# Eight instead of six expert blocks begun before the routing is complete, and their closing sums rearranged over VectorE, ScalarE and GpSimd

## The chip, the cores and the metric

The kernel runs on one core of a Trainium2 chip. The metric is the time of one execution on the device in microseconds. Lower is better. Engines are named as the profile names them: PE is TensorE's matmul side (PEld its weight loads), DVE is VectorE, ACT is ScalarE, POOL is GpSimd, SP is SyncE, which here only issues DMAs.

## The reference, cut to what matters

The reference is a two-layer decoder over x of shape (32, 100, 256), each sub-layer followed by a layer norm. The part that matters here is the last sub-layer, a mixture of eight experts over the 3200 tokens, and the layer norm behind it:

```python
logits = x_flat @ Wg + bg                      # (3200, 8)
probs = jax.nn.softmax(logits, axis=-1)
assignments = jnp.argmax(probs, axis=-1)       # one expert a token
h = jax.nn.gelu(jnp.einsum('nd,edh->neh', x_flat, W1) + b1[None], approximate=False)
eo = jnp.einsum('neh,ehd->ned', h, W2) + b2[None]
selected = jnp.take_along_axis(eo, assignments[:, None, None], axis=1)[:, 0, :]
w = jnp.take_along_axis(probs, assignments[:, None], axis=1)
out = (w * selected).reshape(N, T, d)
...
x = _layernorm(x + out)                        # no gain, no bias
```

## The kernel before, in words

The attention part (two layers, 32 batches each) runs from a plan written out by hand: `at(slot, place, do)` puts a piece of work into a numbered slot, and `run_slots` (L911) issues the slots in order. What is issued in one order stays in that order on each engine (only at the seam between the two contexts, the attention part and the block loop, do instructions of the second slip in between the last of the first). The slots of the last layer end at 347.

While attention still runs, the rows of a batch whose routing is done are scattered by GpSimd to `regions`, a DRAM buffer with room per expert. The experts then work on blocks of 128 rows that belong to one expert. There are 32 blocks (`BLOCKS` = 3200/128 + 7). `BEGUN` = 6 of them are begun early, from what 24 batches have sent (`BEGIN_WITH`): `begun_rows` and `begun_experts` (L860, L870) read their places and experts into registers, `load_begun` (L874) loads rows and first matrix, and `BEGINNING` (L36) gives for each the slot in which its rows are turned (`turn_rows`, two PE transposes and an ACT copy) and the slot of its first matrix (`first_matrix`, eight matmuls and two ACT additions of a bias). The first matrix of the last begun block is left to `end_begun`.

After the last slot come, still in the first context: the load of ACT's table for gelu (L1000), `table_of_others` (the table with the places of the remaining blocks, which SP waits for before it loads them), `end_begun` (L893: for each begun block a gelu on ACT and the second matrix on PE, four matmuls into one of four PSUM banks), and `sum_begun` (L902). For each begun block that calls `share_and_residual` (L135), four DVE instructions:

- L138 adds the expert's second bias and empties the PSUM bank,
- L139 multiplies by the token's share and adds the residual row,
- L141 and L142 make mean and variance.

`margin` (L145, POOL) adds 1e-05 to the variance, `scale` (L148, POOL) takes the power -1/2, `shift_of` (L151, DVE) makes minus mean times that, `normalise_on_scalar` (L1049, ACT) normalises a block with it; `normalise` (L1053, through L154, DVE) does the same on VectorE. `store` scatters the 128 finished rows to the output by an indirect DMA that POOL issues (L779).

The remaining 26 blocks go through a loop (L1061) as a pipeline: in step i the load of block i+10 is issued, the rows of block i+2 are turned, the first matrix of i+1 and its gelu run, block i-3 is normalised on ACT, the second matrix of i and its sums run, and block i-3 is stored. On ACT the order of a step is therefore: copy of turned rows (i+2), gelu (i+1), normalisation (i-3). In the step before the first of these, L1066 puts the ACT normalisations of the begun blocks 0 to 2, after the gelu of the first other block and ahead of the copy for the third. Begun blocks 3 to 5 are normalised on DVE in the steps 8 to 10. At the end of the loop, POOL issues the stores of blocks 26 to 28, then the margin and power of the last pair, then the stores of 29 to 31.

Of the kernel before, what the change touches and what calls it, by code (L numbers as in the profile page):

```python
# [11 lines left out]
I32 = mybir.dt.int32  # L12
# [6 lines left out]
E = 8  # L19
P = 128  # L20
# [13 lines left out]
FILLS = 23  # L34
BEGUN, BEGIN_WITH = 6, 24
BEGINNING = (((338, 1), (340, 2)), ((338, 3), (342, 1)), ((339, 1), (343, 3)), ((339, 3), (345, 2)), ((340, 1), (346, 0)), ((341, 1), None))  # L36
NO_TOKEN = 1000000
# [29 lines left out]
def decoder_kernel(ctx: ExitStack, tc: tile.TileContext, a: dict, out: bass.AP):  # L67
# [66 lines left out]

    def share_and_residual(i, ps, pool):  # L135
        t = blocks[i]
        y = t["y"]
        nc.vector.tensor_tensor(y, ps, b2[:, bass.ds(t["e"], 1), :].rearrange("p o d -> p (o d)"), ALU.add)  # L138
        nc.vector.scalar_tensor_tensor(y, y, t["x"][:, D:D + 1], t["x"][:, :D], ALU.mult, ALU.add)  # L139
        st = pool.tile([P, 6], F32, tag="st", name=f"st_{i}")  # L140
        nc.vector.bn_stats(st, y)  # L141
        nc.vector.bn_aggr(mv_all[:, i, :], st)  # L142

    def margin(i, n):
        nc.gpsimd.tensor_scalar_add(rs_all[:, i:i + n], mv_all[:, i:i + n, 1], 1e-05)  # L145

# [14 lines left out]
    with ExitStack() as att:  # L161
# [649 lines left out]

        def write_table(name, upto, skips, firsts):

            past = sm.tile([32, E - 1], F32, tag="tb_past", name=f"{name}_past")
            col = sm.tile([32, 2], F32, tag="tb_col", name=f"{name}_col")
            nc.vector.tensor_scalar(past, upto[:32, :E - 1], c["steps"][:32, 1:2], None, ALU.is_le)
            nc.vector.tensor_reduce(col[:, 1:2], past, AX.X, ALU.add)
            skips = skips()
            nc.vector.tensor_tensor_reduce(past, past, skips[:32, :E - 1], 1.0, firsts[:32, :], ALU.mult, ALU.add, col[:, 0:1])
            nc.vector.tensor_copy(rows_by_block[:, 0:64:32], col)  # L820
            nc.vector.transpose(table, rows_by_block)

        def table_of_begun():

            assert BEGIN_WITH * S - E * (P - 1) > (BEGUN - 1) * P
            u = {}

            def counts():
                u["n"], u["upto"] = blocks_of_experts("begun", 0.5 / P - 0.5, None)

            def whole_blocks():
                n, upto = u["n"], u["upto"]
                nc.vector.tensor_scalar(upto, upto, float(BEGUN), None, ALU.min)
                nc.vector.tensor_copy(done[:, 0:1], upto[:, 0:1])
                nc.vector.tensor_tensor(done[:, 1:], upto[:, 1:], upto[:, :E - 1], ALU.subtract)
                nc.vector.tensor_scalar(n, done, -float(P), float(B * S), ALU.mult, ALU.add)

            def rows():
                write_table("begun", u["upto"], lambda: u["n"], c["steps"][:, 0:1])

            def for_others():
                nc.vector.tensor_tensor(over, done[:, 1:], done[:, :E - 1], ALU.subtract)
                nc.vector.tensor_scalar(over, over, float(P), float(B * S), ALU.mult, ALU.add)
                nc.vector.scalar_tensor_tensor(first_done, done[:, 0:1], float(P), c["steps"][:, 0:1], ALU.mult, ALU.add)
            return counts, whole_blocks, rows, for_others

        def table_of_others():

            n, upto = blocks_of_experts("counts", 0.5 - 0.5 / P, done)

            def skips():
                nc.vector.scalar_tensor_tensor(n[:, :E - 1], n[:, :E - 1], -float(P), over, ALU.mult, ALU.add)
                return n
            write_table("counts", upto, skips, first_done)

# [4 lines left out]
        def begun_rows():  # L860
            firsts = of_table(0, BEGUN, 0, (ENG.SP,), (BLOCKS_AT_MOST - 1) * P)
            experts = of_table(0, BEGUN, 1, (ENG.SP,), E - 1)
            for i, (first, e) in enumerate(zip(firsts, experts)):
                t = blocks[i]
                t["first"], t["e"], t["ident"] = first, e, ident
                t["x"], t["y"] = x_all[:, i, :], x_all[:, BEGUN + i, :D]
                t["hT"], t["xT"] = slot_of(2 * BEGUN + i), slot_of(3 * BEGUN + i)
                t["w"] = w1_begun[:, i, :]
# [32 lines left out]

        def sum_begun():  # L902
            for i in range(BEGUN):
                share_and_residual(i, blocks[i]["ps"], sm)
                if i == BEGUN // 2 - 1:
                    margin(0, BEGUN // 2)
                    scale(0, BEGUN // 2)
                if i == BEGUN // 2:
                    shift_of(0, BEGUN // 2)

# [91 lines left out]
        end_begun()  # L1002
        sum_begun()

    with ExitStack() as moe:
# [3 lines left out]
        ps_m = moe.enter_context(tc.tile_pool(name="ps_m", bufs=2, space=bass.MemoryType.PSUM))  # L1009
        m16 = moe.enter_context(tc.tile_pool(name="m16", bufs=16))  # L1010
        m12 = moe.enter_context(tc.tile_pool(name="m12", bufs=12))
# [3 lines left out]
        for i in range(BEGUN, BLOCKS):  # L1015
            blocks[i]["y"] = y_all[:, i - BEGUN, :]

# [24 lines left out]
        def second_layer(i):  # L1042
            ps = bank(f"bo_{i}")[:, :D]
            second_matrix(blocks[i], ps, shared)
            share_and_residual(i, ps, m4)

# [7 lines left out]

        def store(i):
            scatter("out", out=out.rearrange("b s d -> (b s) d"),
                    out_offset=bass.IndirectOffsetOnAxis(ap=blocks[i]["x"][:, D + 1:].bitcast(I32), axis=0), in_=blocks[i]["y"],
                    bounds_check=B * S - 1, oob_is_err=False)

        half = BEGUN // 2  # L1060
        for i in range(BEGUN - 10, BLOCKS):  # L1061
# [3 lines left out]
            if i == BEGUN - 1:  # L1065
                for j in range(half):  # L1066
                    normalise_on_scalar(j)
                    store(j)
            if i < BEGUN:
                continue  # L1070
            if i > BEGUN + 2:
                normalise_on_scalar(i - 3)
            second_layer(i)
            if i == BLOCKS - 1:
                normalise_on_scalar(i - 2)
                store(i - 3)
            if i == BEGUN + 1:
                margin(half, half)
                scale(half, half)
            if i % 2:  # L1080
                margin(i - 1, 2)
                scale(i - 1, 2)
            elif i > BEGUN:
                shift_of(i - 2, 2)
            if BEGUN + 1 < i < BEGUN + 2 + half:
                normalise(i - 2 - half)
                store(i - 2 - half)
            if BEGUN + 2 < i < BLOCKS - 1:
                store(i - 3)
        store(BLOCKS - 3)  # L1090
# [73 lines left out]
```

## Time and profile before

| | us |
|---|---|
| three runs | 1735.86, 1736.29, 1737.64 (median 1736.29) |
| the profiled execution, its own time | 1733.78 |
| its span in the profile | 1731.8 |
| PE busy in it | 1678.4 (97%) |
| DVE, POOL, ACT busy | 1296.1, 1096.8, 911.9 |
| stretch behind the last slot, to the last POOL instruction | 1655 to 1725.7 |

The profile is one execution of the program. Its times are counted from the start of the span. A row of the timeline gives start, duration, engine, line, operation and tiles; a bracket at its end says how long the engine had been idle and what ended the wait. The table of windows gives busy time by engine in a stretch, and after them the granted TensorE clock (1.00 is full speed) and the busy share and rate of DMA.

### The profile page before, as it was taken

Reading aid. Unit: us, or ns where it says so; the run is one execution under the profiler, and the core shown is the slowest. Engines: PE = TensorE matmul, PEld = TensorE weight load, DVE = VectorE, ACT = ScalarE, POOL = GpSimd, SP = SyncE. Lnnn points to the kernel's source line nnn. Section 1 sums busy time; section 2 is a strip of 40 time slices with the busy share of each in tenths; the row PEclk is TensorE's granted clock in tenths of the full one; section 3 lists DMA queues with packets and bytes.
Section 4 is the critical chain, followed back from the end, with each engine's and each line's share of the span. In section 5 each row is a group of like instructions: output and inputs, shape, how many; then the busy total and the mean of one; then the engine's idle time right before and its main releaser. Section 6 shows DMA issues by size and latency. Waiting matters only on the chain.

```text
span 1731.8 us, 52249 instructions
## 1 busy us (share of the span) xinstructions
PE 1678.4 (97%) x20803; PEld 1298.7 (75%) x20803; DVE 1296.1 (75%) x3803; ACT 911.9 (53%) x2255; POOL 1096.8 (63%) x1655
## 2 busy tenths in 40 slices
PE   8999999999999999999999999999999999999996
PEld 6777777777777777776777777777777777777685
DVE  5677877777787777787767787877777777786775
ACT  3455555555555555555445555555555555554554
POOL 1566676666667666666336777676766767675657
PEclk9999999999999999999999999999999999999998
DMA  4001322332332233121421131010000000021063
GB/s 161 15 22 31 82 66 64 83 85 50 85 82 65 65 82 85 45 53 31 135 90 55 55 104 47 29 29 19 27 13 22 26 19 20 19 72 56 11 202 123
DMA packets 64048, 104.90 MB, mean 61 GB/s; under 512 B 6108, under 2 KB 43486, under 8 KB 63679
## 3 DMA queue, kind: packets, MB, share of 16 engines
q1 hardware_dynamic: 59790, 94.44, 19.9%
q0 software_dynamic: 3584, 6.59, 1.2%
q8 instruction: 165, 2.70, 0.7%
q14 instruction: 77, 0.62, 0.1%
q10 hardware_dynamic: 432, 0.54, 0.1%
HBM read 61.32 MB, written 41.13 MB: 59 GB/s over the span
## 4 chain that ended last, share of the span: by engine, by line
PE 78%; DVE 14%; POOL 3%; issue 2%; DMA 1%; ACT 0%; POOLq 0%; SPq 0%; DVEq 0%; ACTq 0%
PE r_t_x L435 13%; PE sc_x L341 10%; PE r_k L536 8%; PE r_v L545 7%; PE r_a_x L450 6%; DVE pr L421 6%; PE r_t_s L392 4%; PE r_o_x L364 3%; POOL pr L425 3%; PE r_o_s L364 3%; PE r_qx L321 3%; PE sc_s L341 2%; PE r_a_s L399 2%; DVE pr_s L382 2%; DVE mx_s L379 2%
## 5 line engine op out<-in xcount | busy, mean ns | idle before, releaser
L425 POOL TENSOR_TENSOR pr<-pr,mx_x 100x361 f32<-100x361 f32 x992 | 766.2, 802 | 230.8 <-DVE mx_x L421 223.1
L436 ACT ACTIVATE pT_x<-r_t_x 120x400 f32<-120x400 f32 (+1 forms) x768 | 371.0, 503 | 268.0 <-PE r_t_x L435 265.8
L435 PEld LDWEIGHTS r_t_x<-ident,pr 100*120 100x120 f32 (+1 forms) x3072 | 313.6, 138 | 111.1 <-POOL pr L425 33.8
L435 PE MATMUL r_t_x<-ident,pr 100*120 100x100 f32 (+1 forms) x3072 | 380.4, 252 | 11.4 <-POOL pr L425 10.5
L421 DVE CUSTOM_DVE_ANT_0 pr<-sc_x,dist 100x361 f32<-100x361 f32 x512 | 244.5, 530 | 121.9 <-PE sc_x L341 97.8
L421 DVE CUSTOM_DVE_ANT_0 pr<-sc_x,zero 100x361 f32<-100x361 f32 x512 | 244.4, 529 | 73.9 <-PE sc_x L341 67.2
L341 PE MATMUL sc_x<-kT_x,qz_x 32*100 32x361 f32 x2048 | 221.8, 502 | 7.8 <-DVE mx_x L421 4.5
L96 POOL TENSOR_SCALAR rs_s<-mv_s 100x1 f32<-100x1 f32 x64 | 14.3, 223 | 288.8 <-DVE mv_s L94 260.7
L450 PE MATMUL r_a_x<-pT_x,v_cross 120*32 120x100 f32 (+1 forms) x6144 | 172.2, 252 | 0.0
L379 DVE TENSOR_REDUCE mx_s<-sc_s 100x16 f32<-100x1600 f32 x64 | 116.6, 1822 | 70.1 <-PE sc_s L341 70.1
L538 ACT ACTIVATE kT_x<-r_k,c_columns 128x361 f32<-128x361 f32 x128 | 72.0, 563 | 161.8 <-PE r_k L536 161.8
L450 PEld LDWEIGHTS r_a_x<-pT_x,v_cross 120*32 120x32 f32 (+1 forms) x6144 | 129.9, 110 | 24.4 <-ACT kT_s L485 2.2
L393 ACT ACTIVATE pT_s<-r_t_s 100x400 f32<-100x400 f32 x256 | 112.6, 504 | 28.8 <-PE r_t_s L392 26.3
L382 DVE TENSOR_TENSOR pr_s<-sc_s,mx_s 100x1600 f32<-100x1600 f32 x64 | 116.7, 1824 | 2.2
L392 PE MATMUL r_t_s<-ident,pr_s 100*100 100x100 f32 x1024 | 106.2, 249 | 0.3 <-DVE pr_s L382 0.3
L341 PEld LDWEIGHTS sc_x<-kT_x,qz_x 32*100 32x100 f32 x2048 | 68.2, 159 | 44.4 <-issue 16.1
L545 PE MATMUL r_v<-shared,ctx 128*120 128x256 f32 (+1 forms) x384 | 100.5, 384 | 0.0
L392 PEld LDWEIGHTS r_t_s<-ident,pr_s 100*100 100x100 f32 x1024 | 94.2, 129 | 5.5 <-ACT shared L547 0.7
L547 ACT COPY v_cross<-r_v 120x256 f32<-120x256 f32 x168 | 62.5, 372 | 58.0 <-PE r_v L545 58.0
L332 DVE SCALAR_TENSOR_TENSOR qz_x<-r_qx,qm_x_scale,qm_x_bias 128x400 f32<-128x400 f32 x64 | 37.6, 630 | 69.6 <-PE r_qx L321 69.6
L536 PE MATMUL r_k<-ctx,shared 128*128 128x361 f32 x256 | 88.6, 468 | 0.6 <-DMA ctx<-in_ctxT_dram 0.6
L536 PE MATMUL r_k<-ctx,c_l1x_wk 128*128 128x361 f32 x256 | 89.1, 470 | 0.0
(254 smaller groups left out, 2909.5 us busy)
## 6 DMA issues: line engine op xcount, KB each, us to landing
regions<-no_token SPq DMA_DIRECT2D x23, 1161.0 KB
ctx<-in_ctxT_dram SPq DMA_DIRECT2D x64, 361.0 KB
wb<-in_experts_dram SPq DMA_DIRECT2D x26, 257.0 KB
values_dram<-shared SPq DMA_DIRECT2D x8, 768.0 KB
v_cross<-values_dram SPq DMA_DIRECT2D x8, 768.0 KB
dist<-in_dist_dram SPq DMA_DIRECT2D x32, 141.0 KB
xb<-regions SPq DMA_DIRECT2D x26, 129.0 KB
x_all<-in_x_dram SPq DMA_DIRECT2D x32, 100.0 KB
```

The source lines that it names most:

```text
L341: nc.tensor.matmul(dst, lhsT=qz[rows, p, k, :], rhs=kT[rows, k, :], start=True, stop=True)
L379: nc.vector.tensor_reduce(mx, sg, AX.X, ALU.max)
L382: nc.vector.tensor_tensor(pr, sg, mx.unsqueeze(3).to_broadcast([S, NG, NG, S]), ALU.subtract)
L392: nc.tensor.transpose(pt[:, j, :], t["pr_s"][:, j, g, :], ident[:S, :S])
L393: nc.scalar.activation(t["pT_s"][:, g], pt, AF.Exp)
L421: nc.vector.tensor_tensor_reduce(pr[:, j, :SK], sc[:, j, :], bias, 1.0, LOWEST, ALU.add, ALU.max, mx)
L425: nc.gpsimd.tensor_tensor(pr[:, j, :SK], pr[:, j, :SK], mx.to_broadcast([S, SK]), ALU.subtract)
L435: nc.tensor.transpose(pt[:n, j, :], t["pr_x", g][:, j, k0:k0 + n], ident[:S, :S])
L436: nc.scalar.activation(t["pT_x", g][:n, i], pt[:n], AF.Exp)
L450: nc.tensor.matmul(av[32 * j:32 * j + 32, h, :], lhsT=t["v_x"][:n, i, head(part, j), :], rhs=t["pT_x", part][:n, i, j, :], start=(i == 0), ...
L536: nc.tensor.matmul(ps, lhsT=c[sx + "_wk"][:, k, m * P:(m + 1) * P], rhs=t["ctx"][:, k, :], start=(k == 0), stop=(k == NC2 - 1))
L545: nc.tensor.matmul(ps, lhsT=ctx_b[:, k, k0:k0 + n], rhs=c[sx + "_wv"][:, k, :], start=(k == 0), stop=(k == NC2 - 1))
```

## The change

- `BEGUN` goes from 6 to 8, so that 24 blocks are left for the loop. `BEGINNING` gets the slots of two more blocks: the first matrix of block 5 moves from `end_begun` to slot 346, block 6 is turned in 344 and has its first matrix in 347, block 7 is turned in 345 and has its first matrix in `end_begun`.
- `share_and_residual` is split: `second_bias` (DVE) writes the biased sum into a tile of its own and so empties the bank; the rest follows. For begun blocks y now takes the place of the rows x.
- The begun blocks' sums are reordered: the biases of blocks 0, 1 and 2 first, then in turn the rest of block i and the bias of block i+3.
- `margin` moves from POOL to DVE; margins and powers of begun blocks go by pairs instead of by threes.
- Begun blocks 0 and 1 are normalised on POOL, 2 to 7 on ACT, none on DVE.
- In the loop's end, the power of the last pair is ahead of the store of block 28.
- The table of the begun blocks is made in five planned parts instead of four. A pool for loaded rows goes from 16 to 18 buffers.

```diff
-BEGUN, BEGIN_WITH = 6, 24
-BEGINNING = (((338, 1), (340, 2)), ((338, 3), (342, 1)), ((339, 1), (343, 3)), ((339, 3), (345, 2)), ((340, 1), (346, 0)), ((341, 1), None))
+BEGUN, BEGIN_WITH = 8, 24
+BEGINNING = (((338, 1), (340, 2)), ((338, 3), (342, 1)), ((339, 1), (343, 3)), ((339, 3), (345, 2)),
+             ((340, 1), (346, 0)), ((341, 1), (346, 1)), ((344, 1), (347, 1)), ((345, 2), None))
...
-    def share_and_residual(i, ps, pool):
+    def second_bias(t, ps):
+        nc.vector.tensor_tensor(t["sum"], ps, b2[:, bass.ds(t["e"], 1), :].rearrange("p o d -> p (o d)"), ALU.add)
+
+    def share_and_residual(i, pool):
         t = blocks[i]
         y = t["y"]
-        nc.vector.tensor_tensor(y, ps, b2[:, bass.ds(t["e"], 1), :].rearrange("p o d -> p (o d)"), ALU.add)
-        nc.vector.scalar_tensor_tensor(y, y, t["x"][:, D:D + 1], t["x"][:, :D], ALU.mult, ALU.add)
+        nc.vector.scalar_tensor_tensor(y, t["sum"], t["x"][:, D:D + 1], t["x"][:, :D], ALU.mult, ALU.add)
...
     def margin(i, n):
-        nc.gpsimd.tensor_scalar_add(rs_all[:, i:i + n], mv_all[:, i:i + n, 1], 1e-05)
+        nc.vector.tensor_scalar(rs_all[:, i:i + n], mv_all[:, i:i + n, 1], 1e-05, None, ALU.add)
...
-        def sum_begun():
-            for i in range(BEGUN):
-                share_and_residual(i, blocks[i]["ps"], sm)
-                if i == BEGUN // 2 - 1:
-                    margin(0, BEGUN // 2)
-                    scale(0, BEGUN // 2)
-                if i == BEGUN // 2:
-                    shift_of(0, BEGUN // 2)
+        def sum_first_of_begun():
+
+            for t in blocks[:3]:
+                second_bias(t, t["ps"])
+            for i in range(4):
+                share_and_residual(i, sm)
+                second_bias(blocks[i + 3], blocks[i + 3]["ps"])
+                if i % 2:
+                    margin(i - 1, 2)
+                    scale(i - 1, 2)
+                if i == 1:
+                    for k in range(2):
+                        y = blocks[k]["y"]
+                        nc.gpsimd.tensor_scalar(y, y, mv_all[:, k, 0:1], rs_all[:, k:k + 1], ALU.subtract, ALU.mult)
+                        if k == 0:
+                            store(k)
+            store(1)
+            second_bias(blocks[BEGUN - 1], blocks[BEGUN - 1]["ps"])
...
+        def sum_others_of_begun():
+            for i in range(4, BEGUN):
+                share_and_residual(i, m4)
+                if i % 2:
+                    margin(i - 1, 2)
+                    scale(i - 1, 2)
+                    if i < BEGUN - 1:
+                        store(i - 2)
+                else:
+                    shift_of(i - 2, 2)
+                    if i == 4:
+                        for k in range(2, 4):
+                            normalise_on_scalar(k)
+                        store(2)
+                    else:
+                        normalise_on_scalar(4)
+                        store(4)
...
             if i == BEGUN - 1:
-                for j in range(half):
-                    normalise_on_scalar(j)
-                    store(j)
+                sum_others_of_begun()
             if i < BEGUN:
                 continue
-            if i > BEGUN + 2:
-                normalise_on_scalar(i - 3)
+            normalise_on_scalar(i - 3)
             second_layer(i)
-            if i == BLOCKS - 1:
-                normalise_on_scalar(i - 2)
-                store(i - 3)
-            if i == BEGUN + 1:
-                margin(half, half)
-                scale(half, half)
             if i % 2:
                 margin(i - 1, 2)
                 scale(i - 1, 2)
-            elif i > BEGUN:
+            else:
                 shift_of(i - 2, 2)
-            if BEGUN + 1 < i < BEGUN + 2 + half:
-                normalise(i - 2 - half)
-                store(i - 2 - half)
-            if BEGUN + 2 < i < BLOCKS - 1:
-                store(i - 3)
+            if i == BLOCKS - 1:
+                normalise_on_scalar(i - 2)
+            store(i - 3)
```

## The prediction

> **What bounds the kernel now.** I read the page first: PE is busy 97% of the span, so nearly all of it is attention on PE, which the change leaves alone. All that it touches lies behind 1646 us. I then read the table of windows over that end, the chain of waits from 1657 on, and the timeline of ACT, DVE and POOL there. The windows (length, busy PE, PEld, DVE, ACT, POOL, granted clock, DMA):
>
> ```profile
> 1637.00:1657.00 20.00, 16.07 (x173) 13.78 (x166) 13.04 (x67) 9.92 (x29) 9.17 (x17) 0.99 0.06 17
> 1657.00:1664.00 7.00, 7.00 (x28) 5.89 (x28) 5.86 (x21) 2.15 (x7) 0.95 (x2) 0.78 0.48 135
> 1664.00:1672.00 8.00, 7.38 (x53) 6.54 (x52) 7.05 (x21) 5.30 (x16) 5.02 (x7) 1.00 0.95 293
> 1692.00:1712.00 20.00, 20.00 (x143) 18.40 (x142) 15.86 (x47) 14.96 (x43) 16.41 (x23) 1.00 0.62 186
> ```
>
> Up to 1657 PE has holes (16.07 of 20 busy); in the loop it has none. DVE is busy 7.05 of 8 us at 1664 to 1672: around the begun blocks it is as tight as PE. In 1657 to 1664 the clock was 0.78. The chain:
>
> ```profile
> 1657.09 6.78 PE r_bo L132 x24
> 1664.64 1.14 PE bh L126 x8
> 1666.48 1.46 ACT x_all L1049 x3
> 1668.26 1.16 PE bh L126 x8
> 1669.42 0.87 PE r_bo L132 x4
> ```
>
> The second matrices of the begun blocks, the first other block, then three ACT normalisations of begun blocks, which hold back the third other block's first matrix; after that PE alone, at one block per 1.98 us (the second matrices start at 1671.23, 1673.21, ... in the timeline). Timeline rows that price the parts:
>
> ```profile
> 1653.01 0.33 ACT L309 COPY xT_m<-r_x_m 128x200 f32<-128x200 f32 x1 [0.52 <-PE r_x_m L306]
> 1655.03 1.28 ACT L1000 ACT_TABLE_LOAD   x1
> 1656.32 0.42 ACT L896 ACTIVATE x_all<-x_all 128x256 f32<-128x256 f32 x1
> ...
> 1658.91 0.42 DVE L138 TENSOR_TENSOR x_all<-r_bo,xnT 128x256 f32<-128x256 f32 x1 [0.64 <-PE r_bo L132]
> 1659.37 0.48 DVE L139 SCALAR_TENSOR_TENSOR x_all<-x_all 128x256 f32<-128x256 f32 x1
> 1659.88 0.43 DVE L141 BATCH_NORM_STATS2 st<-x_all 128x6 f32<-128x256 f32 x1
> 1660.35 0.18 DVE L142 BATCH_NORM_AGGREGATE mv_all<-st 128x2 f32<-128x6 f32 x1
> 1660.53 0.43 DVE L138 TENSOR_TENSOR x_all<-r_bo,xnT 128x256 f32<-128x256 f32 x1
> ...
> 1666.37 1.57 ACT L1049 ACTIVATE x_all<-x_all,shift,rs_all 128x256 f32<-128x256 f32 x3
> 1667.85 0.36 ACT L120 COPY bxT<-bt 128x256 f32<-128x256 f32 x1
> ...
> 1720.70 0.24 POOL L145 TENSOR_SCALAR rs_all<-mv_all 128x2 f32<-128x2 f32 x1
> 1721.03 0.72 POOL L148 TENSOR_TENSOR rs_all<-rs_all,mhalf 128x2 f32<-128x2 f32 x1
> ```
>
> The reader is to see: a DVE block costs 1.62 us start to start (0.46 for the bias, 1.16 for the rest), against 1.98 on PE; and ACT takes the copy of turned rows (L120) only behind the normalisations, in order.
>
> **What can be won at most.** From the first bias (1658.91) to the last mean and variance (1719.08) DVE has 60.2 us. Its work there is 32 x 1.63, 13 shifts of 0.13 and three normalisations of about 0.45, 55.3: 4.9 idle. After the change it is 32 x 1.63, 16 margins of about 0.15 and 14 shifts, 56.4. Moving blocks out of the loop takes 1.98 off PE each, but DVE still owes 1.63 for each. So no more than some 4 us is to be had; 0.2% (3.5 us) is about what a measurement of this kernel can tell from no change.
>
> **Part by part** (times as the changed profile would have them).
>
> *Slots 344 to 347.* Two turns (0.22 of PE each by their 0.11 us pitch) and two first matrices (0.90 each) are added. PE has room: the holes from 1651.7 to 1652.6 and from 1653.8 to 1655.2 take the matrices of blocks 5 and 6. ACT is what shows: the biases of block 5 (0.62, L128) now stand ahead of the copy at 1653.01. They follow the copy for block 7 and the biases of block 4 and end at 1653.57: the last batch's routing, the table and SP's loads come 0.56 later. The biases of block 6 (0.62) stand ahead of the table load, which so starts at 1656.2 instead of 1655.03; the first gelu ends at 1657.9, the first second matrix (L132) starts at 1657.95 instead of 1656.88: +1.07. The register loads grow from 6 to 8 values (PE 1.23 and DVE 1.06 us before, some 0.4 more each): PE's lies behind queued matmuls, DVE's in a wait that lasts to 1653.95; with that cover gone, 0.4 each. SP gets four more DMAs (386 KB a block) in slots 327 and 328, ten slots ahead of use, DMA nearly idle there: nothing; were they late, the wait would be at slot 344.
>
> *PE behind that.* Eight second matrices at 0.86 (warm): to 1664.85. Rows of the first other block are there by then (issue to landing 2.6 us). Turn, copy, first matrix as before (0.93 and 0.90, then the next turn, next first matrix): second matrix of block 8 at 1667.87.
>
> *DVE.* Bias 0 at 1659.0, 1 and 2 as PE delivers (1659.9, 1660.75), and only then the rest of block 0, at 1661.2. From there: four rests of 1.17, five biases of 0.46, two margins of 0.15 (bounds 0.13 as a shift and 0.23 as on POOL): 1668.5. Loads of table values between (about 0.5 idle before 1668.49 now): share 4 at 1669.0 to 1670.1, shift for 2 and 3 at 1670.2, share 5, margin, share 6: 1672.8.
>
> *POOL.* Powers at 0.72 to 0.89, stores at 1.27 to 1.40 start to start, two normalisations. No such one is in the trace: below 0.22 (L145, two columns), above 0.80 (L425, 100x361); nearest is L357, 100x256, 0.63 to 0.73: 0.7. The power for 4 and 5 stands behind the store of block 2, which waits for ACT's normalisation at 1670.9: it ends about 1673.1. Hence the shift for 4 at 1673.15. A POOL normalisation of 1.5 would make that 0.7 later.
>
> *The wait this adds.* ACT's order is now: gelu of block 8 (ends 1667.6), normalisations of 2 and 3 (wait for the shift at 1670.2), of 4 (waits for 1673.15, ends 1673.9), then the copy of block 10's turned rows and the gelu of block 9. PE, having done block 8 at 1668.7 and a turn, can do nothing: the first matrix of 10 needs that copy, the second matrix of 9 that gelu. It resumes at 1674.2 and starts block 9's second matrix at about 1675.2, where it now starts at 1673.21. From block 9 on both kernels do the same, bound by PE: **+2.0**. Block by block this comparison already holds what the two blocks fewer save.
>
> *Clock.* Row first: at 1656.88 to 1660.25 the second matrices are 0.427 us apart, then 0.216; one stretch of 3.4 us at half speed, 1.7 us lost, after a stretch in which PE's longest hole was 1.4 us. The Trainium skill (TensorE: Matmul & The Clock Gate, Part 1) says that the clock halves after an idle window of about 3.4 us, free-running, and returns after a busy one. By the rule today's drop wouldn't be, as no hole is that long; by the row sparse work is enough. For the new hole, 1669.0 to 1674.2 with nothing in it, both give a drop, 0.2 to 1.7 by its phase, more if the first warm window is again too sparse; I take the row's **+1.7**. For 1652 to 1658, where holes are filled now, rule and row differ: by the rule 0, by the row 1.7 again. I take 0; the other end is a case below.
>
> *Contention.* Rows: L154 on DVE takes 0.38 beside an idle POOL, 0.60 beside a store. The Trainium skill (GPSIMD Engine Reference, section 4.1) speaks against normalising there: elementwise work belongs on VectorE, though a one-input operation is near line rate; by it the moved step alone costs little. The row makes it 0.2 of DVE for each normalisation and its store: **+0.5**, below 0 excluded, up to 1.
>
> *The end.* POOL is the bound after the last power: margin off POOL saves 0.33 before the last store, and the power of 28 and 29 can start 0.2 earlier (1715.95, not 1716.15). The last power ahead of store 28 changes no sum: POOL has no idle time there, and the margin is ready (1719.3) as store 27 ends. **-0.6**. The margins' 0.15 per pair on DVE lie in its waits for PE (0.3 a block); without them, 0.15 per pair. The first table's five parts, 18 buffers and the unneeded DVE normalisations: hidden under PE now, nothing.
>
> **Sum**: 2.0 + 1.7 + 0.5 - 0.6 = +3.6. The profiled execution took 1733.8 (span 1731.8 and 2.0 around): 1737.4. The median of the runs is 2.5 above the profiled one; I add the difference to the median: 1736.3 + 3.6 = 1739.9.
>
> **Rivals.**
>
> - *The stall as told, clock kept* (17%): +1.9, 1738.2. For: the gate's phase is free. Against: a hole longer than a window.
> - *More is lost* (18%): the clock also drops at the second matrices. DVE now waits for three of them before its first long step, so it loses 1.7 as well, where before it started after one; or POOL's normalisations are slow (0.7). +5 to +7, 1741 to 1743. Against: the filled holes.
> - *No stall, DVE bound* (23%), on the other side: the copy of block 10 isn't held back (it is needed by 1670), PE runs up to four banks ahead, and DVE runs without a wait: block 8's bias at 1674, then 24 blocks of 1.77 end at 1716.6 instead of 1719.1; with the end -3.0, 1733.3, the floor being -4.3. For: before, the same placement cost just 0.55. Against: its shift was made from three blocks' sums and was ready (1665.47) before ACT was free (1666.37); now it needs seven blocks' sums. It decides whether ACT's normalisation of 4 begins before 1670. That the blocks 6 and 7 aren't begun in time (the change not doing what it says) would come out as a wait in slot 344 and fall under "more".
>
> **How the numbers follow.** Forecast 42%, range +2.5 to +5.5: 37 slower, 5 same. Clock kept: 17 same. More lost: 18 slower. No stall: 12 faster, 11 same. So slower 55%, same 33%, faster 12%. The range from 1734.0 to 1743.3 leaves out the lower half of "no stall" and the tail of "more". Slower cases alone: 1738.8 to 1743.
>
> **What would show it.** Right: PE empty for some 5 us from about 1669, released by ACT's L120; on ACT, L1049 waiting for DVE's shift or POOL's power; PEclk below 1 behind it; the first L132 about 1 us later; POOL's last store sooner after the last matmul. Wrong: PE gapless from 1666 on, or DVE without idle time up to 1716; or any difference ahead of 1646.

## The result, and the profile after

The changed kernel takes 1741.47 us (median of 9 runs, 1739.34 to 1743.19) against 1736.70 (9 runs, 1734.37 to 1738.49) before: ratio 1.0029, 95% interval 1.0020 to 1.0037, or 4.8 us slower. Forecast were 1739.9 and a range from 1734.0 to 1743.3.

The profiled execution of the changed kernel has a span of 1739.6 us. Both profiles were aligned on the last attention row that VectorE normalises (1652.12 before, 1654.99 after); "rel" below is the time from that point, in each kernel's own profile. Of the 2.87 us ahead of that point, 2.4 aren't the change's. 1.7 of them are one stretch of 3.41 us at half clock at 908 us, which most profiles of this study have at that place, whatever the kernel, and the one of before happens not to have; the rest, some 0.7, was for the most part there before 908 already, and executions of the kernels below differ by more than that there among themselves.

The other 0.5 is the change's, far ahead of the place that was predicted. It comes near 1550 us, in the middle of attention, where DVE makes the table of the begun blocks. The rows there, the first before and the others after (its line numbers are three higher):

```profile
1549.14 1.82 DVE L379 TENSOR_REDUCE mx_s<-sc_s 100x16 f32<-100x1600 f32 x1 [1.29 <-PE sc_s L341]
1549.84 1.91 DVE L851 TENSOR_TENSOR over<-done 128x7 f32<-128x7 f32 x1
1551.94 1.82 DVE L382 TENSOR_REDUCE mx_s<-sc_s 100x16 f32<-100x1600 f32 x1
1555.67 0.87 PE L344 MATMUL sc_x<-kT_x,qz_x 32*100 32x361 f32 x8 [0.35 <-DVE pr_s L385]
```

With five parts instead of four the last part of the table (`over`) stands one slot later, beside three operations of POOL (1549.44 to 1551.72), and takes 1.91 us where it took 0.74. Before, DVE waited 1.29 us for PE ahead of the next reduction; now the reduction is late, and PE waits 0.35 us. The rows of attention behind it are 0.39 to 0.52 us later in all twelve profiles that have the five parts, experiment 6 with its six begun blocks too, and not in experiment 8, which keeps the four.

The table of windows after (length, busy PE, PEld, DVE, ACT, POOL, granted clock, DMA share, GB/s):

```profile
1637.00:1657.00 20.00, 18.01 (x231) 15.32 (x228) 12.86 (x59) 10.36 (x34) 10.85 (x18) 1.00 0.05 14
1657.00:1664.00 7.00, 6.66 (x36) 6.02 (x36) 4.38 (x27) 5.19 (x14) 1.00 (x1) 0.76 0.13 33
1664.00:1672.00 8.00, 7.67 (x47) 6.82 (x46) 7.23 (x24) 1.30 (x5) 3.34 (x4) 1.00 0.85 247
1672.00:1692.00 20.00, 14.50 (x86) 13.02 (x85) 13.27 (x42) 10.74 (x29) 14.06 (x15) 0.83 0.94 317
1692.00:1712.00 20.00, 20.00 (x143) 18.45 (x142) 16.32 (x52) 14.72 (x42) 14.08 (x15) 1.00 0.57 170
```

The holes up to 1657 are filled, as the change does it (PE 18.01 of 20). The fourth row is where the time went: between 1672 and 1692 PE is busy for 14.50 of 20 us and the mean clock is 0.83. The same stretch before:

```profile
1672.00:1692.00 20.00, 19.96 (x142) 18.21 (x141) 15.99 (x47) 13.50 (x40) 15.69 (x21) 1.00 0.91 308
```

After the change, ACT in the row above that one (1664 to 1672) is busy for 1.30 of 8 us: it is waiting. The chain of waits over that place:

```profile
1676.37 2.07 DMA wb<-in_experts_dram
1678.48 2.08 PE bh L127 x8
1680.55 1.71 PE r_bo L133 x4
1682.26 0.43 PE bt L120 x2
1682.69 1.14 PE bh L127 x8
1683.83 0.87 PE r_bo L133 x4
1684.69 0.22 PE bt L120 x2
1684.91 0.89 PE bh L127 x8
```

The eight records of a first matrix take 2.08 us where they take 0.89 at full clock. (They are four float32 matmuls; the profile has two records for each, and the description of the kernel ahead counts records.) The chain names a DMA of a matrix as the releaser at 1678.48. That is a case in which the chain misleads: the loads that block needs had landed some 9 us before, and the timeline, whose brackets carry the wait, tells another story. Rows of it for ACT, DVE, POOL and PE, a selection, sorted by start:

```profile
1656.36 0.33 ACT L312 COPY xT_m<-r_x_m 128x200 f32<-128x200 f32 x1
1658.93 1.28 ACT L1022 ACT_TABLE_LOAD   x1
1660.22 0.42 ACT L903 ACTIVATE x_all<-x_all 128x256 f32<-128x256 f32 x1
...
1669.19 1.25 POOL L927 TENSOR_SCALAR x_all<-x_all,mv_all,rs_all 128x256 f32<-128x256 f32 x1
1670.74 1.09 POOL L782 DMA_INDIRECT out_dram<-x_all  x1 [0.30 <-POOL x_all L927]
1671.89 1.23 POOL L927 TENSOR_SCALAR x_all<-x_all,mv_all,rs_all 128x256 f32<-128x256 f32 x1
1673.09 0.73 POOL L151 TENSOR_TENSOR rs_all<-rs_all,mhalf 128x2 f32<-128x2 f32 x1
1673.85 0.16 DVE L154 SCALAR_TENSOR_TENSOR shift<-mv_all,rs_all 128x2 f32<-128x2 f32 x1 [1.78 <-POOL rs_all L151]
1674.01 1.10 POOL L782 DMA_INDIRECT out_dram<-x_all  x1 [0.19 <-POOL rs_all L151]
1674.05 1.09 ACT L1072 ACTIVATE x_all<-x_all,shift,rs_all 128x256 f32<-128x256 f32 x2 [2.55 <-DVE shift L154]
1675.41 1.17 POOL L782 DMA_INDIRECT out_dram<-x_all  x1 [0.30 <-ACT x_all L1072]
1676.59 0.74 POOL L151 TENSOR_TENSOR rs_all<-rs_all,mhalf 128x2 f32<-128x2 f32 x1
1677.37 0.16 DVE L154 SCALAR_TENSOR_TENSOR shift<-mv_all,rs_all 128x2 f32<-128x2 f32 x1 [0.95 <-POOL rs_all L151]
1677.57 0.60 ACT L1072 ACTIVATE x_all<-x_all,shift,rs_all 128x256 f32<-128x256 f32 x1 [2.43 <-DVE shift L154]
1678.07 0.35 ACT L121 COPY bxT<-bt 128x256 f32<-128x256 f32 x1
1678.48 2.08 PE L127 MATMUL bh<-bxT,wb 128*128 128x128 f32 x8 [5.50 <-ACT bxT L121]
```

Read from the bottom: PE stood empty for 5.50 us until ACT had copied block 10's turned rows; ACT did that only behind the normalisation of block 4, which waited for DVE's shift, which waited for POOL's power, which stood behind POOL's own two normalisations and three stores. Behind the hole PE runs one block per 1.98 us, as before.

### The profile page after: what moved, and what is told of

The parts are those of the page before. It is cut to its first block, busy times and chain, and to the rows that moved or that the text cites. A ratio compares the mean times of both kernels' runs of the same rounds, so it can differ in the third digit from the quotient of the medians.

```text
span 1739.6 us, 52247 instructions
## 1 busy us (share of the span) xinstructions
PE 1681.5 (97%) x20803; PEld 1302.2 (75%) x20803; DVE 1299.4 (75%) x3817; ACT 914.9 (53%) x2258; POOL 1097.4 (63%) x1643
## 4 chain that ended last, share of the span: by engine, by line
PE 78%; DVE 15%; POOL 3%; issue 2%; DMA 1%; SPq 1%; ACT 0%; POOLq 0%; DVEq 0%; ACTq 0%
PE r_t_x L438 13%; PE sc_x L344 10%; PE r_k L539 8%; PE r_v L548 7%; PE r_a_x L453 6%; DVE pr L424 6%; PE r_t_s L395 4%; PE r_o_x L367 3%; POOL pr L428 3%; PE r_o_s L367 3%; PE r_qx L324 3%; PE r_a_s L402 2%; PE sc_s L344 2%; DVE pr_s L385 2%; DVE mx_s L382 2%
```

## The experiments

Each is an edit of the changed kernel unless said otherwise, and each ratio is to the kernel before. The ratio with its interval is the one on record; it can differ by some 0.0008 from the quotient of the two medians printed beside it, and the comparisons go by the ratio.

**1. The normalisations behind the copy.** ACT's normalisations of the begun blocks 2 to 7 leave their place ahead of the copy; they and their stores come some steps later in the loop, in some steps two at a time.

```diff
-                    if i == 4:
-                        for k in range(2, 4):
-                            normalise_on_scalar(k)
-                        store(2)
...
+        later = {8: (), 9: (), 10: (2, 3), 11: (4,), 12: (5, 6), 13: (7,), 14: (8,), 15: (9, 10), 16: (11,), 17: (12, 13),
+                 18: (14,), 19: (15, 16)}
...
-            normalise_on_scalar(i - 3)
+            finished = later.get(i, (i - 3,))
+            for k in finished:
+                normalise_on_scalar(k)
```

> The changed kernel with one edit: on ACT the normalisations of begun blocks 2 to 7 (and their stores on POOL) come two to seven steps of the block loop later, the lag is made up for by two normalisations in every other step until step 19; DVE's and PE's work and POOL's two normalisations stay. Theory (the hole in PE is made by ACT's order: the copy of block 10's turned rows stands behind normalisations that wait for DVE's shift and POOL's power): the 5.5 us wait of PE for L121 goes, the clock stays 1.00 behind 1670, about 5 to 7 us less than the changed kernel, that is 1.5 to 2.5 us below before (ratio 0.9985 to 0.9992). Rival A (DVE is the bound there, and PE would only run ahead and then wait at the four PSUM banks): PE stops later instead, waiting for DVE's bias, and the time is within 1 us of the changed kernel (1.0025 to 1.003). Rival B (the front of the stretch, slots 344 to 347, makes the loss): unchanged, 1.003.

Measured: 1738.68 against 1737.99, ratio 1.0001 (0.9992 to 1.0009). The hole is gone: PE runs from block 8 on without a gap, block 9's second matrix at rel 18.76 (25.36 in the changed kernel). So it was those normalisations, in their place ahead of the copy, that made it. The time is a miss (0.9985 to 0.9992 were expected): the kernel is only level with the one before, for a new hole stands at blocks 20 to 22. ACT and PE there, in the timeline of this kernel:

```profile
1698.17 0.60 ACT L1072 ACTIVATE y_all<-y_all,shift,rs_all 128x256 f32<-128x256 f32 x1 [2.67 <-DVE shift L154]
1699.08 1.48 PE L127 MATMUL bh<-bxT,wb 128*128 128x128 f32 x8 [2.30 <-ACT y_all L1072]
```

The same kind of wait, later: POOL stood idle early (1.55 and 2.67 us ahead of two powers) as the stores came late, and then had too little slack to catch up. A store costs it 1.27 to 1.40 us start to start and a power about 0.95, some 3.6 of the 3.96 us in which PE does two blocks. The hole also took the clock again (3.41 us at half speed from 1699.76).

**2. No normalisation on POOL.** Blocks 0 and 1 go to ACT, still ahead of the copy; the stores of 0 to 2 go behind the power for 4 and 5.

```diff
-                if i == 1:
-                    for k in range(2):
-                        y = blocks[k]["y"]
-                        nc.gpsimd.tensor_scalar(y, y, mv_all[:, k, 0:1], rs_all[:, k:k + 1], ALU.subtract, ALU.mult)
...
+            shift_of(0, 2)
...
-                        for k in range(2, 4):
+                        for k in range(4):
                             normalise_on_scalar(k)
```

> The changed kernel with one edit: blocks 0 and 1 are normalised on ACT like 2 and 3, not on POOL, and the stores of 0 to 2 stand behind the power of blocks 4 and 5 on POOL; the ACT normalisations keep their place ahead of block 10's copy. Theory with POOL's two normalisations (1.25 and 1.23 us in the trace) as the part of the hole that was mis-sized: DVE's shift no longer waits for POOL (1.78 and 0.95 us), the hole is about 2 us shorter, two more normalisations on ACT take back 0, since ACT waits anyway; the clock still drops: about 2 us less than the changed kernel (ratio about 1.0015 to 1.002). Rival (DVE alone sets the shift): hole as long as before within 0.5 us, 1.003. If POOL were the whole cause, the hole would be gone and the time that of before.

Measured: 1739.62 against 1737.99, ratio 1.0012 (1.0004 to 1.0020). Block 9's second matrix comes at rel 22.89 instead of 25.36, with one stretch at half clock instead of two. PE's hole is 3.10 us instead of 5.50. POOL's two normalisations and the stores 0 to 2, which this edit takes from ahead of the powers together, are thus a good part of the hole; the run does not separate the one from the other. The power for 6 and 7 now stood behind five stores, and that made a second hole, 1.23 us of PE, which the expectation did not have:

```profile
1681.46 0.16 DVE L154 SCALAR_TENSOR_TENSOR shift<-mv_all,rs_all 128x2 f32<-128x2 f32 x1 [4.04 <-issue]
1681.65 0.60 ACT L1066 ACTIVATE x_all<-x_all,shift,rs_all 128x256 f32<-128x256 f32 x1 [3.48 <-DVE shift L154]
```

**3. The hole filled with 44 matmuls of the identity by itself**, ahead of block 10's first matrix, to hold the clock up.

```diff
+            if i == BEGUN + 2:
+                for _ in range(44):
+                    nc.tensor.matmul(ps[:, 0, :], lhsT=ident, rhs=ident, start=True, stop=True)
```

> The changed kernel with one edit: 44 extra matmuls (identity by identity, 0.11 us each, about 4.9 us) on PE in the hole, ahead of block 10's first matrix; what they write is written over by it. Theory with the clock as a part of its own: the hole keeps its end (ACT's copy), the granted clock stays 1.00 behind it, the first matrix of 10 takes 1.1 and not 2.1 us: 1.5 to 2.3 us less than the changed kernel (ratio 1.0015 to 1.002). Rival (the clock costs nothing because DVE or ACT bound the blocks behind the hole): no change, 1.003. Rival (PE has no slack at all): 4.9 us more.

Measured: 1743.34 against 1737.99, ratio 1.0028 (1.0017 to 1.0039). A miss in size: each float32 matmul is two records here, so 44 of them took 9.99 us and PE was free again some 4 us after it had been needed. The clock stayed at 1.00. That the kernel is no slower than the changed one though PE resumed 3.2 us later (rel 26.6 against 23.5) says that the clock matters, but not how much.

**4. Experiments 1 and 2 together**, blocks 0 and 1 on ACT in the loop's first step.

```diff
-        later = {8: (), 9: (), 10: (2, 3), ...
+        later = {8: (0, 1), 9: (), 10: (2, 3), ...
```

> The two edits of the late normalisations and of the empty POOL together: as the first kernel of this set, and blocks 0 and 1 normalised on ACT in step 8 of the loop, none on POOL. Theory: no hole; against the first kernel DVE's steps beside POOL (1.09 for two L142, 0.74 for two L144) are freed and no wait for POOL's power is left, 0.3 to 1 us less, if anything of DVE's lateness still reaches PE or the end: 2 to 3 us below before (ratio 0.998 to 0.9988). Rival A (DVE bound): as for the first kernel, no gain over the changed one beyond POOL's 2 us.

Measured: 1738.31 against 1737.99, ratio 1.0002 (0.9994 to 1.0010), a miss. It is no better than experiment 1: PE has gaps ahead of blocks 17, 21, 23 and 24. POOL starts its stores still later here; taking work off it doesn't help when what it waits for comes late.

**5. The hole filled with 24 matmuls**, the right size this time.

> The changed kernel with 24 extra matmuls on PE (0.22 us each as the trace of the 44 shows them, 5.4 us in all) ahead of block 10's first matrix; what they write is written over. The 44 took 9.8 us and ended 4.3 us behind ACT's copy, which hid their effect. Theory: PE is busy up to the copy, the clock stays 1.00, the first matrix of 10 and the second of 9 take 1.1 and 0.9 us instead of 2.1 and 1.7: block 10's second matrix about 2 us sooner than in the changed kernel, ratio 1.0015 to 1.002. Rival (DVE and POOL, late by then, bound the end whatever PE's clock): last store within 0.5 us of the changed kernel's, 1.0025 to 1.003.

Measured: 1738.89 against 1736.06, ratio 1.0014 (1.0007 to 1.0021). PE in the timeline, and the window that was 14.50 busy at clock 0.83 in the changed kernel:

```profile
1672.18 5.52 PE L1065 MATMUL bh<-ident 128*128 128x128 f32 x48
1677.83 1.16 PE L127 MATMUL bh<-bxT,wb 128*128 128x128 f32 x8
```

```profile
1672.00:1692.00 20.00, 19.88 (x152) 18.63 (x151) 14.95 (x49) 12.49 (x34) 15.44 (x18) 1.00 0.96 327
```

The wait is as long as it was, the clock is full, and the loss falls from 4.8 to 2.8 us (by the ratios from 0.29% to 0.14%). Some half of it was the clock (by the two intervals, anything from a small part to most).

**6. Six blocks begun**, with everything else of the change.

```diff
-BEGUN, BEGIN_WITH = 8, 24
+BEGUN, BEGIN_WITH = 6, 24
...
+            share_and_residual(4, m4)
+            shift_of(2, 2)
+            normalise_on_scalar(2)
+            store(2)
+            share_and_residual(5, m4)
+            margin(4, 2)
+            scale(4, 2)
```

> The changed kernel with six begun blocks again (the slots of before), and everything else of the change: biases of three blocks first, margins on DVE, blocks 0 and 1 normalised on POOL, 2 ahead of the copy on ACT, last power ahead of a store. Theory: a hole is still made, since the normalisation of 2 waits for the shift made behind POOL's two normalisations and the sums of block 4, but it ends with block 2 and not with 4, so about 3 us shorter than 5.5, and its place is a block earlier: last store +0.5 to +2 against before, ratio 1.0003 to 1.0012. Rival (two blocks more begun are the loss by themselves, through the front): ratio 0.9995 to 1.0000. Rival (the order of the sums is the loss, whatever the count): 1.0025 to 1.003.

Measured: 1741.52 against 1736.06, ratio 1.0026 (1.0017 to 1.0034). A miss of the theory, in the range of the second rival: with six blocks the loss is about whole. ACT waits longer for one shift, and the hole is there at 3.31 us:

```profile
1674.98 0.60 ACT L1072 ACTIVATE x_all<-x_all,shift,rs_all 128x256 f32<-128x256 f32 x1 [3.89 <-DVE shift L153]
1675.89 1.16 PE L126 MATMUL bh<-bxT,wb 128*128 128x128 f32 x8 [3.31 <-ACT bxT L120]
```

So the loss doesn't need two more blocks. It comes from how the sums are laid over the engines: ACT's normalisations ahead of a copy that PE needs, and POOL's work ahead of the power that those normalisations need.

**7. POOL fed early.** No normalisation on POOL; the power for 0 and 1 at once, their normalisations on ACT in the last begun step, behind the copy of block 9; the stores of 0 and 1 around the next power; the later blocks six steps behind instead of three, caught up in the steps 12, 16 and 20.

```diff
+                if i == 1:
+                    scale(0, 2)
+                if i == 2:
+                    shift_of(0, 2)
...
+            store(0)
+            scale(2, 2)
+            store(1)
...
+        later = {8: (2,), 9: (3,), 10: (4,), 11: (5,), 12: (6, 7), 13: (8,), 14: (9,), 15: (10,), 16: (11, 12), 17: (13,),
+                 18: (14,), 19: (15,), 20: (16, 17)}
...
+                if i == BEGUN - 1 and d == 2:
+                    normalise_on_scalar(0)
+                    normalise_on_scalar(1)
```

> A version made from the readings: the changed kernel with no normalisation on POOL; blocks 0 and 1 normalised on ACT between the copy of block 9's rows and the gelu of block 8 (a place where ACT waits for PE), their stores before and behind the power of 2 and 3, all later ones six steps behind in the loop and catching up by one at the steps 12, 16 and 20, so that POOL starts its stores early and never has two stores more than it can take. Theory (PE's hole by ACT's order, and behind it POOL as the next bound: stores of 1.27 us and powers of 0.95 fill it): no hole in PE, no gap of POOL above 1 us, last store about 2 us sooner than before measured from the last normalised row of attention: ratio 0.9985 to 0.9993. Rival (POOL fills up again as in the two late kernels): 0.9998 to 1.0005. Rival (DVE bound): 1.000 with DVE's gaps at zero.

Measured: 1734.19 against 1736.06, ratio 0.9989 (0.9982 to 0.9995): faster than the kernel before, and so than the changed one. The time is in the expected range, the profile only in part: POOL has a gap of 2.62 us, and the last store comes 0.84 us sooner than before (rel 71.76), not 2. Its windows:

```profile
1672.00:1692.00 20.00, 20.00 (x144) 18.51 (x143) 17.15 (x57) 15.53 (x43) 14.13 (x15) 1.00 1.01 323
1692.00:1712.00 20.00, 18.66 (x128) 16.55 (x127) 16.76 (x52) 13.47 (x41) 16.57 (x19) 1.00 0.65 209
```

PE is full where the hole was (20.00 of 20). It loses 1.3 us in the second row, in gaps ahead of blocks 22, 23 and 25.

**8. The kernel before, with only the margins on DVE and the last pair's power ahead of the store of block 28.**

```diff
-        nc.gpsimd.tensor_scalar_add(rs_all[:, i:i + n], mv_all[:, i:i + n, 1], 1e-05)
+        nc.vector.tensor_scalar(rs_all[:, i:i + n], mv_all[:, i:i + n, 1], 1e-05, None, ALU.add)
```

> The kernel before with two parts of the change alone: margins on DVE, and the last pair's power ahead of the store of block 28. Theory: the end gets 0.4 to 0.6 us shorter from the last second matrix to the last store (9.03 us before, 8.65 in the changed kernel), the loop stays bound by PE: ratio 0.9995 to 1.0000, not to be told from none by the times. Rival (0.15 us of DVE a pair delays ACT's normalisations): 1.0003 or more, with waits of L1049 for DVE in the loop.

Measured: 1735.50 against 1736.06, ratio 0.9994 (0.9984 to 1.0003): not to be told from no change. Its profile has 8.66 us from the last second matrix to the last store, before 9.03.

**9. Experiment 7 with the stores ahead of the power in every step**, since POOL waited there for a margin with a store ready behind it.

```diff
+            if i < BLOCKS - 1:
+                for k in finished:
+                    store(k)
             if i == BEGUN:
-                store(2)
                 scale(6, 2)
-                finished = ()
```

> The early version (ratio 0.9989) with one edit: in every step of the loop but the last the stores of finished blocks stand on POOL ahead of the step's power, not behind it. In the early version POOL waited 2.62 us for the margin of blocks 8 and 9 with the store of block 3 ready behind it, and PE then lost about 2 us at blocks 18 to 21 waiting for ACT, DVE's shift and in the end POOL's power. Theory (POOL is the bound behind the hole): the 2.6 us gap goes, the holes in PE at blocks 18 to 21 go or shrink, last store 1 to 2 us sooner from the last normalised row of attention (71.76 us in the early version): ratio 0.9978 to 0.9986. Rival (a power that is later by two stores delays DVE's shift and so ACT and PE): 0.999 to 1.0005. Rival (PE is the bound now): 0.9988 as the early version.

Measured: 1736.29 against 1737.81, ratio 0.9990 (0.9982 to 0.9999). A miss: POOL's gap shrank from 2.6 to 1.4 us, and the time is that of experiment 7. In the trace of experiment 7 the gaps stand ahead of blocks 22, 23 and 25, not at 18 to 21 as the expectation has it. PE's gaps now stand ahead of blocks 17, 18 and 22, so they are not made by that wait of POOL.

**10. One first matrix later**, block 5's in slot 347 instead of 346, so that it doesn't stand ahead of the copy xT_m of the last batch.

```diff
-((341, 1), (346, 1)), ((344, 1), (347, 1))
+((341, 1), (347, 0)), ((344, 1), (347, 1))
```

> The changed kernel with the first matrix of block 5 behind the turning of the last batch's rows (slot 347, place 0) and not ahead of it (346, place 1), so that ACT's two biases of it follow the copy of the turned rows. Theory of the front: from the last normalised row of attention to that copy 0.9 us as before (1.37 in the changed kernel), to the router's matmul the same 0.3 to 0.5 sooner; to the first second matrix 0 to 0.4 sooner, since the biases are then before the table load of ACT all the same. Rival (the copy is late for another reason): unchanged at 1.37. The hole behind and its length are as in the changed kernel; one look, the time says nothing.

Measured: 1741.26 in its one run. The copy comes at rel 0.96 instead of 1.37, as it should. The last router comes at 1.68 instead of 1.75, for now the matrix stands in its way on PE. The copy's delay cost nearly nothing.

**11. Experiment 7 with the catching up in other steps**, to see whether ACT's double steps make the gaps that are left.

```diff
-        later = {..., 12: (6, 7), ..., 16: (11, 12), ..., 20: (16, 17)}
+        later = {..., 13: (7, 8), ..., 18: (13, 14), ..., 23: (19, 20)}
```

> The kernel of the sixth-step lag (no normalisation on GpSimd, begun blocks 0 and 1 on ScalarE, later ones six steps behind), with only the steps moved in which ScalarE catches up by doing two normalisations: 13, 18 and 23 instead of 12, 16 and 20. Theory A (a double step makes the copy of turned rows late and so makes the gap on TensorE): the gaps of 0.2 to 1 us that stood at blocks 17 to 22 move to about 14-15, 19-20 and 24-25, each one to two blocks behind a double step, and blocks 16 and 17 run at 1.98 us; ratio to before 0.998 to 1.000. Rival B (GpSimd's stores and powers are the bound, and the gap is a normalisation that waits for a shift of VectorE behind a late power): gaps stay at 17 to 22 or grow, as stores come later, with ScalarE waiting for the shift ahead of them; ratio 0.9995 to 1.001.

Measured: 1735.14 against 1737.15, ratio 0.9987 (0.9980 to 0.9993). The gaps stand ahead of blocks 23 and 24; behind the double steps 13 and 18 there are none, and ahead of the gaps no wait of ACT for a shift over 0.6 us. (In experiment 7 they were ahead of 22, 23 and 25, not at 17 to 22.) Neither theory holds.

**12. Experiment 7 with four matmuls of the identity ahead of the last router**, where PE waits 0.76 us.

```diff
+                if l and b == B - 1:
+                    for _ in range(4):
+                        nc.tensor.matmul(ps[:, :P], lhsT=ident, rhs=ident, start=True, stop=True)
```

> The kernel of the six-step lag as it was (double steps 12, 16, 20), with four matmuls of the identity by itself (0.22 us each, 0.88 in all, their result unused) ahead of the last batch's router, where TensorE waits 0.76 us for ScalarE's copy xT_m. Theory A (the clock falls at the second matrices because the stretch before them has too few dense matmuls): with them the stretch of 3.41 us at half clock near the first second matrix is gone from the profile, the second matrices are 0.216 us apart from the first on, and 1 to 1.7 us is won less 0.1 to 0.2 for a router that starts later; ratio to before 0.9978 to 0.9986. Rival B (four are too few, or the drop is given by something else): the stretch at half clock stays, the router is 0.1 to 0.2 late; ratio 0.9985 to 0.9997.

Measured: 1737.42 against 1737.15 in 13 runs, ratio 0.9994 (0.9986 to 1.0003): a miss in time, not better than experiment 7. In the profile the theory's picture is there: the stretch at half clock near the begun blocks' second matrices is gone, they are 0.86 us a block apart from the second on, the router isn't late (rel 1.75), and block 8's second matrix comes at rel 15.73, 1.0 us sooner than in experiment 7. Three other profiles (experiments 3, 5 and 10) lack that stretch without such a filler (3 and 5 run the changed kernel's own instructions up to there), so one profile doesn't prove the filler's part. And the 1.0 us didn't reach the end: in this kernel PE had more gaps, ahead of blocks 17, 18, 21, 22 and 24. One of ACT's stops ahead of them:

```profile
1685.82 0.37 ACT L121 COPY bxT<-bt 128x256 f32<-128x256 f32 x1 [1.65 <-PE r_bo L133]
```

The rows it copies had been turned by 1684.06, and in the steps before it the copy follows the turn within 0.9 us. The transfers aren't late either: by the bytes that the load queue had moved, each matrix of these blocks was there 7 us or more before its use. What holds ACT for about 1 to 1.9 us in a few steps of experiments 7, 9, 11 and 12 stays open.

## Why the prediction was right, and what was mis-sized

**The mechanism.** The step "the wait this adds" is what the trace shows: PE empty from the end of block 8 and one turn on, for 5.50 us (predicted 5.2), released by ACT's copy (L121) behind L1072, with the clock below 1 after it. Experiment 1 took the cause away, and the hole with it. The rival "no stall, DVE bound" fell with its condition: it asked that the normalisation of 4 begin before 1670 in before's time; it began at 1677.57, or 1674.70 in that time.

**The sum, term by term**, from rel times in the two profiles. The last store is 4.9 us later (rel 77.52 against 72.60), and with the 0.5 ahead of rel 0 5.4; the runs say 4.8, with an interval from 3.5 to 6.4.

| term | predicted | measured |
|---|---|---|
| PE resumes with block 10's first matrix | +2.0, and +0.5 of contention | +3.3 |
| half clock behind the hole | +1.7 | +2.3 |
| last second matrix to last store | -0.6 | -0.4 |
| a gap of 0.3 ahead of block 15, only in before's profile | none | -0.3 |
| the table in five parts, near 1550 us | none | +0.5 |
| sum | +3.6 | +5.4 |

- *The resumption* was mis-sized by POOL's two normalisations: 1.25 and 1.23 us against the 0.7 that was taken from the nearest row. POOL has no idle time over 0.30 us from the power for 0 and 1 (1668.19) to the one for 4 and 5 (1676.59), so what is longer there passes on whole: two of them 0.5 longer are 1.1 later. The prediction's warning ("1.5 would make that 0.7 later") had the direction, but too small a size. The other 0.2 is the first second matrix, 1.27 later instead of 1.07. Choosing the nearest row by shape (100x256, L357) was the mistake: L357 is another operation. Here the Trainium skill (GPSIMD Engine Reference, section 4.1) calls one-input elementwise work on GpSimd "roughly line-rate"; the trace doesn't agree, for DVE takes 0.38 to 0.60 for the same operation (L154 of the kernel before, 128x256 with two scalars a partition).
- *The contention* of 0.5 isn't there as such. DVE's L142 takes 0.48 beside a normalisation of POOL (1670.08), and 0.54 and 0.53 beside two of the stores. What held DVE there were waits for POOL's power, 1.78 and 0.95 us. That the 0.5 made up for some of what the resumption was short by is luck.
- *The table in five parts* was put at nothing ("hidden under PE now"), and "any difference ahead of 1646" was named as a sign of being wrong. There is one, 0.5 near 1550 us, by the rows shown with the result: the wait of DVE that hid the table before (1.29 us) no longer covers it. No run changes this part alone; that it is the table rests on these rows and on the twelve profiles against two.
- *The clock* fell for two stretches, 6.83 us, not one; of these PE had work in the last 4.6, so 2.3 are lost. The prediction named that end ("more if the first warm window is again too sparse") and took one. The clock drop at the first second matrices was taken as 0 for the new kernel, by the rule of the Trainium skill (TensorE: Matmul & The Clock Gate, Part 1) that an idle window is needed; it came all the same, 3.41 us at 1659.18, ahead of which PE's longest hole was 0.8 us. As before has it too, it makes little of the difference, and experiments 3 and 5, with the same instructions up to there, don't have it. There the row should have been followed, not the rule.
- *The end* was right in kind, -0.4 for -0.6. Experiment 8 has the same 0.4 by itself, too little to show in a time.
- *The front*: the copy xT_m came 0.47 later (0.56), the first second matrix 1.27 (1.07).
- *What can be won at most*, some 4 us, still stands: experiment 7 got 1.9 of it, with the same eight blocks begun.

The chances put 55% on slower. In number the result, +4.8, lies nearer to the lower end of the rival "more is lost" (+5 to +7) than to the forecast of +3.6. That rival named POOL's slow normalisations, which made 1.1 of the excess; the clock drop that it named, at the second matrices, is in both profiles.

## What to carry to other kernels

An operation on an in-order engine costs what stands behind it: before placing one ahead of work that the bottleneck engine needs, follow its inputs back through every queue, and add the durations there for the exact operation, not for one of like shape. That holds for small operations too: one on 128x7 numbers, moved by one slot, goes with a loss of 0.5 us here. A hole on PE has a second price, the clock behind it; filling the hole with useless matmuls tells the two apart. If an engine off the critical path has little slack (POOL here, some 0.4 us per pair of blocks), letting it start early can do more than taking work from it: experiments 1 and 4 are level with each other, and experiment 7 is faster.

## What the runs showed of the hardware that was not expected

- TensorE's clock halves without an idle stretch: in the changed kernel 3.41 us at half speed from 1659.18, when PE by the records had been busy for 2.32 of the 3.41 us before and had no hole over 0.8 us.
- Within each profile these stretches start whole multiples of 3.413 us apart (in the changed kernel at 908.25, 1659.18 and 1676.25, which are 220 and 5 steps). Whether the clock halves near 1659 differs between executions of the same instructions: in experiments 3 and 5 it doesn't. PE is busy for 68% and 87% of the step in question there, and for 68% in the changed kernel, so the busy share in the records doesn't decide it; what does stays open.
- After a hole of 5.50 us it stayed down for 6.83 us, two such stretches: in the first PE was busy for 1.19 us, in the second throughout. The holes of 2.30, 3.10 and 3.31 us in experiments 1, 2 and 6 cost one.
- A normalisation by two scalars a partition (128x256, float32) takes 1.22 to 1.25 us on GpSimd, 0.60 on ScalarE (as scale and bias) and 0.38 to 0.60 on VectorE.
- A float32 matmul of 128x128 by 128 columns is two records of 0.11 us pitch: 24 matmuls took 5.52 us, 44 took 9.99.
- GpSimd's indirect store of 128 rows holds its queue for 0.97 to 1.30 us (mostly under 1.10) and 0.2 to 0.3 more before the next: two stores and a power are some 3.6 of the 3.96 us that TensorE takes for two blocks.
- A VectorE operation on 128x7 numbers took 1.88 to 1.91 us in all twelve profiles in which it overlaps three GpSimd operations on 100x361 numbers, ending as the last of them ends, and 0.74 in the two in which it overlaps hardly more than one. The reason is not shown.
